# A two-layer graph network on one Trainium2 core: scatters without waits among themselves, an earlier clear of the sorted table, a smaller-stepped fill of the weights' table, deeper loads of terms

## Chip, cores and metric

The kernel runs on one core of a Trainium2 chip, as one launch. The metric is the device time of that core in microseconds; the figure for a kernel is the median over its runs. A profiled execution, recorded separately, gives the trace from which the views below are taken.

## What is computed

The reference has four parts, one after the other, on 6,250 nodes with 256 features and 100,000 edges sorted by destination:

```
x = x + GAT(layernorm(x), edges)            # 8 heads: softmax over incoming edges of exp(leaky_relu(..)), weighted sum
x = x + experts(layernorm(x))               # each node picks 1 of 32 experts: relu(relu(x W1 + b1) W2 + b2)
x = x + RGCN(layernorm(x), edges)           # T[n, rel] = x_n W_rel for 16 relations; sum over edges of T[src, rel] * weight
x = x + FFN(layernorm(x))                   # 2 of 8 experts, chosen once for all nodes, gelu, then a layer norm
```

The layer norms have no learned scale except the last one. Everything is float32.

## The kernel before

**Stages.** A preparation turns the edge lists into per-edge index columns. A *projection* loop over 13 blocks of four 128-node tiles (49 tiles in all) computes the attention projection and stores it in the DRAM table `H_tab`; the per-node terms of the destinations go to `ad_tab`. Then a long loop over 98 *groups* of 1,024 edges does the attention (GAT): GpSimd gathers the source rows of a group with eight indirect DMAs (`gather`, L444, tile `hs`, four buffers), SyncE (SP) loads the destination terms (`load_terms`, L476, four small DMAs per group into one of the tiles `aw`), ScalarE's queue loads the destinations (`load_dst`, tile `db`), and TensorE, VectorE (DVE) and ScalarE (ACT) turn them into sums in a ring of 16 tiles.

**The second layer runs inside the first.** The nodes are cut into three chunks of 6, 16 and 27 tiles. As soon as the ring holds finished sums, a chunk goes through four generators: `take` (normalise, write `x1_tab`), `route` (choose the expert, compute each node's slot in a table sorted by expert, scatter the rows there: L870, table `x_sort`), `experts` (load sorted rows and the expert's weights from `w_tab`, write `y_sort`) and `products` (gather back from `y_sort`, L952; multiply with the 16 relation matrices `wr`, L998; write `T_tab`, L1012). In each turn of the group loop `fill` runs a few steps of these, by a budget of TensorE and DVE time. A loop after the last group runs what is left. Then come the RGCN (98 groups, gathers from `T_tab`, also L444, tile `ts`) and the final FFN.

**What sets the order.** Group loop and remainder lie in `tc.manual_schedule()`: each engine and queue executes its instructions in the order in which the program wrote them.[...] Outside, a planner orders instructions by priority and readiness.

**What the change touches.** The scatters of `route`: 49 indirect DMAs on GpSimd, all writing `x_sort`; each source tile `xs2` (four buffers) is loaded from `x1_tab` by SP three tiles ahead (L113). The generator `Flow.consts`, of which one step runs per group: it fills `w_tab` (one row block per expert: W1, W2, b2 as the 65th row of the W2 part, b1 as last column, the rest zero), then clears `x_sort` (58 stores of 256 KB, four a step), then loads `wr`. `route` may scatter only when `self.ready` is set, after all clears. In `experts`, `ys` has two buffers. All three chunks share one `x_sort`, so a chunk waits until the one before has read its rows.

```
            for c in range(zero.shape[0] // P):
                nc.sync.dma_start(zero[c * P : (c + 1) * P, :], zr)
                if c % 4 == 3:
                    yield
            self.ready = True
```

Of the kernel before, what the change touches and what calls it, by code (L numbers as in the profile page):

```python
# [15 lines left out]
AX = mybir.AxisListType  # L16
DVE = mybir.EngineType.DVE
# [5 lines left out]
P = 128  # L23
# [6 lines left out]
T = 8  # L30
# [16 lines left out]
def gnn_ffn_kernel(  # L47
# [84 lines left out]
    nc.vector.memset(ones, 1.0)  # L132
    eps = const.tile([P, 1], F32, name="eps")
# [6 lines left out]
    dst_f = const.tile([P, T, NG], F32, name="dst_f")  # L140
# [22 lines left out]
    w_tab = dram.tile([E1, P, B1C + 4], F32, name="w_tab")  # L163
# [3 lines left out]
    class Chunk:  # L167


        def __init__(self, a, b, x_sort=None):  # L170
# [3 lines left out]
            if x_sort is None:  # L174
                self.x_sort = dram.tile([self.xt * P, 2 * D], F32, name=f"x_sort{a}_{b}")
            self.y_sort = dram.tile([self.xt * P, D], F32, name=f"y_sort{a}_{b}")
# [4 lines left out]
    whole = Chunk(0, NT)  # L181

# [41 lines left out]
    with tc.tile_pool(name="prep", bufs=1) as prep, tc.tile_pool(name="prep_p", bufs=1, space=PSUM) as prep_p:  # L224
# [72 lines left out]
        for a, o in ((dgf, dst_f), (srf, src_i), (i1f, idx1), (nat["ew"], ew_sb)):  # L297
            for h in range(2):
# [5 lines left out]
                if a is dgf:  # L304
                    nc.vector.tensor_tensor(
                        rlm[:, h * w : (h + 1) * w, :].rearrange("p (q u) g -> p q u g", u=QT),
                        pt.rearrange("p (q u) g -> p q u g", u=QT),
                        lo4[:, h * Q // 2 : (h + 1) * Q // 2, None, :].to_broadcast([P, Q // 2, QT, NG]), ALU.subtract)
                if h == 0:
# [38 lines left out]
    with tc.tile_pool(name="ga", bufs=2) as pa, tc.tile_pool(name="ga1", bufs=1) as pa1, \  # L348
# [16 lines left out]
        for t0, n, r in blocks:  # L365
# [16 lines left out]
            node_dma(nc.scalar, hb, H_tab, t0, n, r, True)  # L382

# [20 lines left out]
    class Group:  # L404


        def __init__(self, pool, g, dynamic):
# [9 lines left out]
            for o, a in ((ii[:, 0], src_i), (ii[:, 1], idx1), (fw[:, 0], dst_f), (fw[:, 1], ew_sb)):  # L417
                nc.vector.tensor_copy(o.rearrange("p (t o) -> p t o", o=1), a[:, :, ds(g, 1)])
            self.di = pool.tile([P, T], I32, name="d_di")
            nc.vector.tensor_copy(self.di, fw[:, 0, :])  # L420
# [38 lines left out]
        def load_dst(self):  # L459

            n = GE if self.dynamic else QT * P
            self.db = self.pool.tile([P, n], I32, name="db", bufs=1 if self.dynamic else 2)
# [191 lines left out]
    class Flow:  # L654


        def __init__(self, es, bufs, psum_bufs):

            self.open, self.bufs = 0, 1
            self.ready = False  # L660
# [13 lines left out]
        def consts(self, zero):  # L674

            yield
# [9 lines left out]
            zr = self.rt.tile([P, 2 * D], F32, name="xs2", bufs=4)  # L686
            nc.vector.memset(zr, 0.0)
# [4 lines left out]
            nc.sync.dma_start(w_tab.rearrange("e p w -> p e w"), zr[:, None, : B1C + 4].to_broadcast([P, E1, B1C + 4]))  # L692
            for k in range(KC):
                nc.sync.dma_start(w_tab[:, :, k * H1 : (k + 1) * H1], f1_w1[:, k * P : (k + 1) * P, :])
            nc.sync.dma_start(w_tab[:, :H1, W2C:B1C], f1_w2)
            nc.sync.dma_start(w_tab[:, H1, W2C:B1C], f1_b2)
            nc.sync.dma_start(w_tab[:, :H1, B1C], f1_b1)
            yield
            for c in range(zero.shape[0] // P):
                nc.sync.dma_start(zero[c * P : (c + 1) * P, :], zr)  # L700
                if c % 4 == 3:
                    yield
            self.ready = True
            for r in range(NREL):
                nc.sync.dma_start(self.wr[:, :, r, :], rel_w[r].rearrange("(k p) o -> p k o", p=P))
                if r % 2 == 1:
                    yield
# [50 lines left out]
        def route(self, ck):  # L758
# [94 lines left out]
            while not (ck.free() and self.ready):  # L853
# [14 lines left out]
            for j in range(ck.nt):  # L868
                r, xs2 = ahead.pop(0)
                nc.gpsimd.indirect_dma_start(  # L870
                    out=ck.x_sort[:, :], out_offset=bass.IndirectOffsetOnAxis(ap=ck.slot[:r, j : j + 1], axis=0),
                    in_=xs2[:r, :], in_offset=None)
                if j + 3 < ck.nt:
# [4 lines left out]
        def experts(self, ck):  # L878
# [7 lines left out]
            for s in range(np_ + 5):  # L886
                if 4 <= s < np_ + 4:
# [5 lines left out]
                    ys = pool.tile([P, 2, D], F32, name="ys", bufs=2)  # L893
# [24 lines left out]
                if 2 <= s < np_ + 2:  # L918
                    lv = live[s - 2]
                    for j in range(lv["n"]):  # L920
                        w = pool.tile([P, B1C + 4], F32, name="w", bufs=6)
                        nc.sync.dma_start(w, w_tab[ds(lv["e"][j], 1)].rearrange("o p w -> (o p) w"))
                        lv["w"].append(w)
                if s < np_:
# [3 lines left out]
                    nc.sync.dma_start(xs[:, :n, :], xs_rows[:, c : c + n, :])  # L928
# [120 lines left out]
    with ExitStack() as es_flow:  # L1049
# [6 lines left out]
        aws = [pr1.tile([P, Q, 2 * HEADS], F32, name=f"aw{i}") for i in range(3)]  # L1056
# [51 lines left out]
        with tc.manual_schedule():  # L1108

            boot = flow.consts(chunks[0].x_sort)  # L1110
            groups = [Group(pg, g, False) for g in range(NG)]
            for g in range(2):
                groups[g].load_dst()
# [264 lines left out]
```

## Time and profile before

| | us |
|---|---|
| median of 3 runs (3813.27 to 3839.88) | 3828.43 |
| the profiled execution, its own time | 3459.76 |
| its span, first to last instruction | 3458.0 |
| projection and preparation, to the first gather | 0 to 114.5 |
| GAT loop, from first to last gather of `hs` | 114.5 to 1287.9 |
| scatters of chunk 0; of chunk 1; of chunk 2 | 416 to 433; 786 to 848; 1358 to 1452 |
| experts of chunk 2, then its products | 1461 to 1600, then to about 2025 |
| RGCN gathers | 2026 to 3019 |
| final FFN | 3019 to 3458 |

The shares of busy time over the whole span (TensorE 70%, GpSimd 50%, DVE 31%, ACT 23%) hide that each stage has another limit. They are read by windows: the mean granted TensorE clock is 0.727 over the span, 1.00 in the products of chunk 2, and about 0.5 where TensorE waits a lot.

In the views, "PE" is TensorE's matmuls, "POOL" is GpSimd, a "q" behind an engine's name is its sequencer, and `x <- y` behind an idle time names what ended it. An indirect DMA counts as busy time of POOL[...]; the data land later.

### The profile page before, as it was taken

Reading aid. Unit: us, or ns where it says so; the run is one execution under the profiler, and the core shown is the slowest. Engines: PE = TensorE matmul, PEld = TensorE weight load, DVE = VectorE, ACT = ScalarE, POOL = GpSimd, SP = SyncE. Lnnn points to the kernel's source line nnn. Section 1 sums busy time; section 2 is a strip of 40 time slices with the busy share of each in tenths; the row PEclk is TensorE's granted clock in tenths of the full one; section 3 lists DMA queues with packets and bytes.
Section 4 is the critical chain, followed back from the end, with each engine's and each line's share of the span. In section 5 each row is a group of like instructions: output and inputs, shape, how many; then the busy total and the mean of one; then the engine's idle time right before and its main releaser. Section 6 shows DMA issues by size and latency. Waiting matters only on the chain. (4 is left out here: it accounts for less than half of the span.)

```text
span 3458.0 us, 32167 instructions
## 1 busy us (share of the span) xinstructions
PE 2423.5 (70%) x8917; PEld 1186.0 (34%) x8918; DVE 1069.1 (31%) x2879; ACT 803.6 (23%) x1684; POOL 1713.0 (50%) x1736
## 2 busy tenths in 40 slices
PE   5334457791675987188999966666666666689997
PEld 4212235341453443054444421111111111166665
DVE  7324646562555653011000002121121211242222
ACT  2112223440333443033333310000000000012332
POOL 0447676774757771200000047777777777622222
PEclk9655576885676999589999975555555555569999
DMA  4697687675886774586444453333333333310000
GB/s 146 193 217 244 186 278 229 200 227 177 265 264 186 227 219 161 169 264 219 168 171 170 159 188 105 105 105 105 105 105 105 105 105 105 89 28 19 19 19 20
DMA packets 326688, 533.40 MB, mean 154 GB/s; under 512 B 84966, under 2 KB 182564, under 8 KB 326496
## 3 DMA queue, kind: packets, MB, share of 16 engines
q1 hardware_dynamic: 218060, 277.92, 24.4%
q0 software_dynamic: 83152, 233.62, 23.7%
q10 hardware_dynamic: 25284, 19.67, 1.9%
q8 instruction: 75, 1.23, 0.2%
q14 instruction: 117, 0.96, 0.1%
HBM read 342.80 MB, written 192.42 MB: 155 GB/s over the span
## 5 line engine op out<-in xcount | busy, mean ns | idle before, releaser
L444 POOL DMA_INDIRECT hs<-H_tab,src_i x784 | 765.7, 977 | 428.3 <-issue 212.0
L444 POOL DMA_INDIRECT ts<-T_tab,idx x784 | 743.7, 949 | 330.4 <-issue 238.5
L998 PE MATMUL pb<-wr,xTt 128*128 128x512 f32 (+1 forms) x1568 | 722.2, 617 | 18.6 <-ACT tr L1001 14.1
L502 PE MATMUL qagg<-ts,oh 128*32 128x256 f32 x1568 | 504.6, 630 | 327.7 <-DMA ts<-T_tab,idx 324.0
L998 PEld LDWEIGHTS pb<-wr,xTt 128*128 128x128 f32 (+1 forms) x1568 | 303.9, 198 | 387.8 <-issue 356.7
L502 PEld LDWEIGHTS qagg<-ts,oh 128*32 128x32 f32 x1568 | 90.2, 139 | 719.9 <-DMA ts<-T_tab,idx 640.4
L1001 ACT COPY tr<-pb 128x512 f32<-128x512 f32 (+1 forms) x392 | 228.4, 587 | 452.7 <-PE pb L998 344.1
L509 ACT COPY qs<-qagg 128x264 f32<-128x264 f32 (+1 forms) x196 | 73.9, 377 | 1117.0 <-PE qagg L502 1095.3
L454 DVE TENSOR_TENSOR oh<-iota,rlm 128x256 f32<-128x256 f32 x196 | 83.1, 425 | 799.2 <-PE qagg L502 793.5
L518 PE MATMUL agg<-qs,pl 128*128 128x264 f32 (+1 forms) x392 | 204.4, 619 | 146.2 <-DVE pl L511 81.9
L557 PE MATMUL pe<-aw,oT 128*128 128x64 f32 x392 | 86.4, 362 | 296.2 <-issue 140.0
L952 POOL DMA_INDIRECT yg<-y_sort,slot x49 | 47.1, 961 | 489.0 <-ACT xl L717 291.6
L579 DVE TENSOR_TENSOR hs<-hs,pe 128x2048 f32<-128x2048 f32 x98 | 223.2, 2277 | 0.0
L557 PEld LDWEIGHTS pe<-aw,oT 128*128 128x128 f32 x392 | 76.5, 267 | 339.6 <-issue 247.9
L1328 PE MATMUL ph<-xT,we 128*128 128x512 f32 (+1 forms) x416 | 177.4, 584 | 15.1 <-DMA we<-in_L_ffn_W_dram,ix 11.7
L518 PEld LDWEIGHTS agg<-qs,pl 128*128 128x128 f32 x392 | 91.2, 280 | 270.5 <-ACT qs L509 162.6
L1336 PE MATMUL po<-we,hid 128*128 128x256 f32 (+1 forms) x784 | 171.9, 379 | 0.5 <-DVE we L1314 0.3
L1336 PEld LDWEIGHTS po<-we,hid 128*128 128x128 f32 (+1 forms) x784 | 148.4, 190 | 26.8 <-issue 5.7
L502 PE MATMUL qagg<-hs,oh 128*32 128x264 f32 x1568 | 155.7, 533 | 0.0
L894 DVE SCALAR_TENSOR_TENSOR ys<-pb,xs 128x512 f32<-128x512 f32 (+1 forms) x72 | 49.2, 684 | 324.8 <-PE pb L892 180.0
L904 PE MATMUL pb<-xTe,w 128*64 128x128 f32 x568 | 99.6, 326 | 40.1 <-DMA w<-w_tab 35.3
L915 PE MATMUL pt<-ident,xs 128*128 128x128 f32 x284 | 58.7, 341 | 95.6 <-DMA xs<-x_sort 92.7
(278 smaller groups left out, 2303.7 us busy)
## 6 DMA issues: line engine op xcount, KB each, us to landing
T_tab<-tr SPq DMA_DIRECT2D x384, 256.0 KB
xs<-x_sort SPq DMA_DIRECT2D x70, 512.0 KB
w<-w_tab SPq DMA_DIRECT2D x142, 194.0 KB
y_sort<-ys SPq DMA_DIRECT2D x70, 256.0 KB
x_sort<-xs SPq DMA_DIRECT2D x58, 256.0 KB
db<-in_dst_dram ACTq DMA_DIRECT2D x392, 32.0 KB
hs<-H_tab,src_i POOLq DMA_INDIRECT x784
ts<-T_tab,idx POOLq DMA_INDIRECT x784
```

The source lines that it names most:

```text
L444: nc.gpsimd.indirect_dma_start(out=hs[:, t, :], out_offset=None, in_=table, in_offset=bass.IndirectOffsetOnAxis(ap=idx(t), axis=0))
L454: nc.vector.tensor_tensor(oh, iota[:, None, :n].to_broadcast([P, T, n]), column(self.rl), ALU.is_equal)
L502: nc.tensor.matmul(ps[q * QW : (q + 1) * QW, :width], lhsT=oh[:, t, :], rhs=vals[:, t, :width], start=u == 0, stop=u == QT - 1)
L509: nc.scalar.copy(qs, ps[:, :width])
L518: nc.tensor.matmul(ps[:, :width], lhsT=pl, rhs=qs, start=True, stop=True)
L557: nc.tensor.matmul(pq[:, u * w : (u + 1) * w], lhsT=oT[:, u, :], rhs=aw.rearrange("p q h -> p (q h)"), start=True, stop=True)
L579: nc.vector.tensor_tensor(hv, hv, pv.to_broadcast([P, T, HEADS, HD]), ALU.mult)
L904: nc.tensor.matmul(ph[:H1, j * P : (j + 1) * P], lhsT=lv["w"][j][:, k * H1 : (k + 1) * H1], rhs=xT[:, k, j * P : (j + 1) * P], start=k == ...
L998: nc.tensor.matmul(pr[:r, :], lhsT=xT[:, k, j * P : j * P + r], rhs=self.wr[:, k, q0 : q0 + 2, :], start=k == 0, stop=k == KC - 1)
L1001: nc.scalar.copy(o2, pr[:r, :])
L1328: nc.tensor.matmul(ph[:, :nn], lhsT=we1[:, i, k, c * P : (c + 1) * P], rhs=xT[:, k, :nn], start=k == 0, stop=k == KC - 1)
L1336: nc.tensor.matmul(po[:r, :], lhsT=hid[:, i, c, j * P : j * P + r], rhs=we2[:, i, c, :], start=i + c == 0, stop=i + c == NFC)
```

## The change

Seven edits. (1) The 49 scatters are told not to depend on other scatters of the same chunk, and every load of sorted rows in `experts` is made to wait for all scatters of its chunk. (2) The written-out order of the group loop and of the remainder binds TensorE, DVE, ACT and SP, no longer GpSimd, whose instructions the planner places. (3) The clears of `x_sort` come from a constant tile of zeros, 128 columns wide and repeated four times along a row; three are issued in each block of the projection, one more along with each load of a relation matrix, and the rest after these. `route` asks for as many cleared tiles as its chunk has. (4) `w_tab` is not zeroed; it is filled in eight steps, two for each quarter of the experts (8 of 32). The rows below the 64 used ones get copies of W2 and b1, and b2 then overwrites one of them. Its rows are 385 columns, not 388. (5) Terms `aw` have six tiles, not three, and are loaded four groups ahead, not two; destinations `db` have three buffers, loaded three groups ahead. (6) `ys` has three buffers. (7) `dst_f`, used only in a branch for wide groups, is not kept; the branch loads it from DRAM.

```diff
@@ constants @@
+    zeros = const.tile([P, P], F32, name="zeros")
+    nc.vector.memset(zeros, 0.0)
-    dst_f = const.tile([P, T, NG], F32, name="dst_f")
-    w_tab = dram.tile([E1, P, B1C + 4], F32, name="w_tab")
+    w_tab = dram.tile([E1, P, B1C + 1], F32, name="w_tab")
@@ new class @@
+    class Clear:
+        def __init__(self, table):
+            self.rows, self.n, self.done = table.rearrange("(c p) (k w) -> c p k w", p=P, w=P), table.shape[0] // P, 0
+        def step(self, n):
+            for c in range(self.done, min(self.done + n, self.n)):
+                nc.sync.dma_start(self.rows[c], zeros[:, None, :].to_broadcast([P, 2 * D // P, P]))
+            self.done = min(self.done + n, self.n)
+    cleared = Clear(chunks[0].x_sort)
@@ projection, end of a block @@
             node_dma(nc.scalar, hb, H_tab, t0, n, r, True)
+            cleared.step(3)
@@ load_dst @@
-            self.db = self.pool.tile([P, n], I32, name="db", bufs=1 if self.dynamic else 2)
+            self.db = self.pool.tile([P, n], I32, name="db", bufs=1 if self.dynamic else 3)
@@ Flow.consts @@
-            nc.sync.dma_start(w_tab.rearrange("e p w -> p e w"), zr[:, None, : B1C + 4].to_broadcast([P, E1, B1C + 4]))
-            for k in range(KC):
-                nc.sync.dma_start(w_tab[:, :, k * H1 : (k + 1) * H1], f1_w1[:, k * P : (k + 1) * P, :])
-            nc.sync.dma_start(w_tab[:, :H1, W2C:B1C], f1_w2)
-            nc.sync.dma_start(w_tab[:, H1, W2C:B1C], f1_b2)
-            nc.sync.dma_start(w_tab[:, :H1, B1C], f1_b1)
-            yield
-            for c in range(zero.shape[0] // P):
...
-            self.ready = True
+            for e in range(0, E1, E1 // 4):
+                es = slice(e, e + E1 // 4)
+                for k in range(KC):
+                    nc.sync.dma_start(w_tab[es, :, k * H1 : (k + 1) * H1], f1_w1[es, k * P : (k + 1) * P, :])
+                nc.sync.dma_start(w_tab[es, :H1, W2C:B1C], f1_w2[es])
+                yield
+                nc.sync.dma_start(w_tab[es, H1:, W2C:B1C], f1_w2[es])
+                nc.sync.dma_start(w_tab[es, H1, W2C:B1C], f1_b2[es])
+                for rows in (slice(0, H1), slice(H1, P)):
+                    nc.sync.dma_start(w_tab[es, rows, B1C], f1_b1[es])
+                yield
             for r in range(NREL):
                 nc.sync.dma_start(self.wr[:, :, r, :], rel_w[r].rearrange("(k p) o -> p k o", p=P))
-                if r % 2 == 1:
-                    yield
+                clear.step(1)
+                yield
+            while clear.done < clear.n:
+                clear.step(1)
+                yield
@@ route @@
-            while not (ck.free() and self.ready):
+            while not (ck.free() and self.clear.done >= ck.xt):
                 yield None
...
-                nc.gpsimd.indirect_dma_start(
+                ins = nc.gpsimd.indirect_dma_start(
                     out=ck.x_sort[:, :], out_offset=bass.IndirectOffsetOnAxis(ap=ck.slot[:r, j : j + 1], axis=0),
                     in_=xs2[:r, :], in_offset=None)
+                ck.put.append(ins.ins)
+                tc.declare_no_dep(ins.ins, group=ck.key, reason="no two nodes share a slot")
+                tc.add_to_no_dep_group(ck.key, ins.ins)
@@ experts @@
-                    ys = pool.tile([P, 2, D], F32, name="ys", bufs=2)
+                    ys = pool.tile([P, 2, D], F32, name="ys", bufs=3)
...
-                    nc.sync.dma_start(xs[:, :n, :], xs_rows[:, c : c + n, :])
+                    ins = nc.sync.dma_start(xs[:, :n, :], xs_rows[:, c : c + n, :])
+                    for put in ck.put:
+                        tc.add_manual_dep(ins.ins, put.name, mybir.DependencyInfo(
+                            mybir.DependencyClass.Sync, mybir.DependencyReason.DATA), reason="all rows are there")
@@ group loop @@
-        aws = [pr1.tile([P, Q, 2 * HEADS], F32, name=f"aw{i}") for i in range(3)]
+        aws = [pr1.tile([P, Q, 2 * HEADS], F32, name=f"aw{i}") for i in range(6)]
-        with tc.manual_schedule():
+        with tc.manual_schedule(engines={PE, DVE, ACT, SP}):
...
-            for g in range(2):
-                groups[g].load_dst()
-                groups[g].load_terms(aws[g % 3])
+            for g in range(4):
+                if g < 3:
+                    groups[g].load_dst()
+                groups[g].load_terms(aws[g])
...
-                if g + 2 < NG:
-                    groups[g + 2].load_dst()
-                    groups[g + 2].load_terms(aws[(g + 2) % 3])
+                if g + 3 < NG:
+                    groups[g + 3].load_dst()
+                if g + 4 < NG:
+                    groups[g + 4].load_terms(aws[(g + 4) % 6])
...
-        with tc.manual_schedule():
+        with tc.manual_schedule(engines={PE, DVE, ACT, SP}):
             while takes or routes or runs or tails:
```

## Prediction

> **What bounds the kernel now.** The whole-span shares decide nothing here, so I read the busy time by stages first, cutting at the scatters that the timeline of GpSimd shows. Columns: stretch, its length, then busy time and count for PE, weight loads, DVE, ACT and POOL, the granted clock, DMA share, GB/s.
>
> ```profile
> 177.00:213.00 36.00, 3.01 (x20) 1.53 (x20) 0.31 (x1) 0.31 (x2) 0.89 (x2) 0.50 1.10 155
> 213.00:416.00 203.00, 101.14 (x542) 53.86 (x542) 117.54 (x250) 52.39 (x131) 154.47 (x160) 0.54 0.76 234
> ...
> 786.00:848.00 62.00, 10.97 (x68) 5.62 (x68) 8.50 (x16) 3.97 (x13) 22.87 (x24) 0.57 0.50 153
> ...
> 1358.00:1461.00 103.00, 20.27 (x38) 8.34 (x38) 0.59 (x4) 6.28 (x11) 26.60 (x27) 0.58 0.45 148
> 1461.00:1600.00 139.00, 114.83 (x510) 73.76 (x511) 19.86 (x33) 43.44 (x103) 0.00 (x0) 0.86 0.84 265
> 1600.00:2025.00 425.00, 416.11 (x1018) 186.56 (x1016) 22.39 (x120) 162.97 (x295) 26.25 (x27) 1.00 0.45 165
> ```
>
> From 213 to 416 GpSimd issues 160 gathers in 203 us, 1.27 us each, while PE, DVE and ACT are busy half the time or less: the rate of gathers sets the pace. In three stretches (177 to 213, 786 to 848, 1358 to 1461) no engine does much. Next the table of waits (total, times, longest):
>
> ```profile
> POOL x_sort L870 <- DMA x_sort<-xs,slot: 102.1, 41, 3.7
> ...
> PE pe L557 <- DMA aw<-ad_tab: 80.7, 7, 44.4
> DVE ys L894 <- DMA y_sort<-ys: 78.8, 14, 9.8
> ...
> POOL hs L444 <- PE qagg L502: 73.8, 18, 35.1
> ```
>
> Every scatter waits for the one before, 102.1/41 = 2.49 us each. The timelines place the others:
>
> ```profile
> 209.54 1.09 PE L557 MATMUL pe<-aw,oT 128*128 128x64 f32 x4 [44.44 <-DMA aw<-ad_tab]
> ...
> 212.93 1.01 POOL L444 DMA_INDIRECT hs<-H_tab,src_i  x1 [35.11 <-PE qagg L502]
> ...
> 1358.23 0.99 POOL L870 DMA_INDIRECT x_sort<-xs,slot  x1 [39.15 <-DVE le L850]
> 1362.15 0.98 POOL L870 DMA_INDIRECT x_sort<-xs,slot  x1 [2.93 <-DMA x_sort<-xs,slot]
> 1365.63 0.96 POOL L870 DMA_INDIRECT x_sort<-xs,slot  x1 [2.50 <-DMA x_sort<-xs,slot]
> ```
>
> At 209 TensorE has waited 44 us for terms that SP queued behind the fill of `w_tab`; GpSimd then lacks free `hs` buffers for 35 us. From 1358 all 27 scatters of chunk 2 stand on the path: the experts cannot begin before them, and after the experts TensorE is full (416 of 425 us), so time won here reaches the end. The RGCN (784 gathers over 993 us) and the final FFN are not touched.
>
> **What the Trainium skill says.** "DMA: Bandwidth & Descriptors", section "Anatomy of one DMA — SWDGE (gpsimd) path", puts some 2 us of fixed cost on such a DMA, most of it confirmation of the write. The trace agrees: 2.0 to 3.7 us between the end of one scatter's issue and the next. The section "Two DMAs through the same engine are not ordered" says that only a completion semaphore orders two transfers; hence the loads of sorted rows must still wait for all scatters. The trace has that wait (SP at L928, 36.4 us in 3 waits). The section "Why a DMA increments its semaphore by 16 and not by 1" says that a transfer uses the largest number of engines up to 16 that divides the outer dimensions: quarters of 8 experts would run on 8 engines where 32 gave 16. No run so far shows such a transfer.
>
> **The parts, in us of the profiled execution.**
>
> *Chunk 2's scatters.* First to last start: 1358.23 to 1450.38, 92.2 us for 26 steps, 3.54 each. Without the wait a step cannot be shorter than GpSimd's 0.96 + 0.30 = 1.26, so 33 us. The next limit is `xs2`: four buffers, each loaded (SP issue 0.4; landing about 2, an estimate from the scatter's like wait), scattered (0.96) and landed (2.5) before reuse: about 6 us by four is 1.5 a step, 39 us. SP also puts `T_tab` stores between loads, and two of these held it 4 us each (1382.8 to 1387.0, 1411.2 to 1415.5). I take 44: **48 saved**, bounds 35 and 58.
>
> *Start of the loop.* Terms now go four groups ahead, ahead of all filling. The wait of 35.1 should go; I take **28**, bounds 8 and 35. What may return is the fill: it loses 6.2 MB of zeros, gains 2 MB of copies, and becomes 28 DMAs instead of 6. Before, W1, W2 and b2 held SP's queue from 175.67 to 198.2 with 4 MB. On half the engines, with copies, that may be 22.5 x 2 x 1.5 = 68 us of queue, and each b2 row waits for the copy it overwrites (four times perhaps 6). Spread over eight groups of 10 us, some 90 us stands against 80; four groups of lead cover the 10 us deficit. If the cover fails, TensorE waits for `aw` again; that is the lower bound.
>
> *Scatters of chunks 0 and 1.* Chunk 0: 416.34 to 432.30 is 16.0 for 5 steps, 6.3 at 1.26. Chunk 1: 61.3 for 15 steps and 8 gathers in between, 29.0 at 1.26. Excess 9.7 + 32.3 = 42. Gathers may now fill gaps. The `xs2` limit keeps a part if they do not: 20 x 0.25 = 5. I take **34**, bounds 15 and 42.
>
> *Experts of chunks 0 and 1.* GpSimd waits for `qagg` 14.9 us between 434 and 600 and 22.6 us between 848 and 1060; in the same windows DVE waits 23.0 and 22.5 for stores of `ys`. A third `ys` buffer and `db` one group earlier (same 392 DMAs on ACT) remove the DVE wait, not the matmuls. **18**, bounds 0 and 38. *Experts of chunk 2:* the remaining 78.8 - 45.5 = 33 us of that wait lie in a stage where DMA runs at 0.84 and 265 GB/s, so I take **4**, bounds 0 and 15; next late are the loads.
>
> *Clears.* 13 blocks x 3 = 39 stores move to the projection: 39 x 0.26 MB = 10.2 MB. SP issues one in 0.42 us, 16 us in all, with only 14 `xin` loads of 0.4 us and four edge loads beside it. At the 265 GB/s seen in the experts they are 39 us of DMA, 32 at its share of 0.84. The first 30 us have a DMA share of 0.28 and the next 85 of 0.48, so 66 us are free: they fit. In pieces of 512 B they may be slower. Placed early, they delay the first `xin`; placed late, the last `H_tab` stores. Cost **6**, bounds 0 and 35. Where they leave the loop GpSimd was the limit anyway, so nothing is gained there; the cover is GpSimd's 1.27 us a gather. The relation loads, one a group, are the same 16.
>
> *The rest:* two copies of `dst_f` (about 0.5 us each by like rows) against one memset; rows of 385 columns, 1% less to load; the wait of the sorted loads for all scatters was there already. Nothing.
>
> Sum: 48 + 28 + 34 + 18 + 4 - 6 = **126**, against the profiled 3459.76: about 3334. The median of the timed runs is 369 us above that execution, and the profile doesn't show where. If TensorE runs slower there, the GAT loop is nearer to TensorE's limit and the terms inside it are worth less, while those at 177 and 1358, where TensorE idles, stay. I carry the sum over nearly whole: 3828 - 123 = **3705**.
>
> **The rivals.**
>
> *The consumers bind.* In the GAT loop PE is 80 to 88% busy from 1060 to 1290 (185 of 230 us). If the loop runs at PE's and DVE's pace, waits of GpSimd are only exchanged for waits on `hs` buffers, and of the loop's 80 us about 6 remain. For: 18 waits on `qagg` exist already. Against: in 213 to 416 and at 786 PE starves. Time: 48 + 6 + 4 - 6 = 52, 3776.
>
> *The change is hidden or does not act:* if scatters still wait (for the shared semaphore, or for `xs2`), 28 + 18 + 4 - 6 = 44 remain, 3784.
>
> *More:* all upper bounds but half, no cost of clears: about 180, 3648.
>
> *Slower.* GpSimd's order is no longer written out, and it is the stage's bound, so any wait that the planner puts in front of gathers goes straight to the end. There are 14 such places in the loop: three batches of scatters and about eleven pairs of `yg` gathers. The trace shows what such an instruction waits when its partner is not ready: 39.15 us (on `le`) and 26.5 us (`yg` on `xl`), today after the last gather, where nothing is queued behind. At 12 us a place the loss is 168, net 42: 3870. It decides from 126/14 = 9 us a place, about one group. For: planner and chip may differ. Against: today these places wait 0.3 us, and with a written order gathers are just as stuck.
>
> **How the numbers follow.** Chances: forecast 0.58, more 0.07, consumers bind 0.17, does not act 0.07, slower 0.11. The range 3630 to 3805 takes in the forecast's bounds and the two weaker gains; beyond it lie the slower case and a little of the better one. The measurement tells about 1% (38 us) from no change. Faster by over 1%, below 3790: nearly all of the forecast and more (0.64), and most of the two weak cases (0.17), 0.81. Slower by over 1%, above 3867: half of the slower case and a tail of unpriced effects, 0.09. Within: 0.10.
>
> **What would show it.** Scatters of chunk 2 about 1.5 us apart; the wait of L870 on scatters near zero; no 35 us gap of GpSimd before 215; last `hs` gather near 1215; TensorE idle less than 45 us before the experts of chunk 2; first gather before 121. The forecast is wrong if waits of `hs` on `qagg` grow by what L870 loses, if GpSimd waits before `yg` or a scatter with gathers behind it, or if the first gather comes after 140.

## The result and the profile after

The kernel after takes 3768.49 us (median of 4 runs, 3767.10 to 3778.74) where before takes 3825.55 (4 runs): a ratio of 0.9855, interval 0.9816 to 0.9895. The gain is 57 us; 123 were forecast.

Two kinds of chip have to be kept apart first, because they answer differently. On **kind A** before takes 3818 to 3828 us (medians): all timed runs up to this result, and the trace of after. On **kind B** it takes 3448 to 3460: the profiled execution that the prediction was worked from belongs here. Each chip showed one kind only, but none served at two times, so the chip and the occasion are not told apart. Every ratio below is against before on the same chip. One late run of before (e16) fell on kind A, its span 3816.3, so the change can be followed there in a pair of traces. The pair on B is e1 (before) and e5 (after). A group of edges is marked by the start of ScalarE's copy of its sums (`qs`), read from the traces.

| us from the start | A before | A after | difference | B before | B after | difference |
|---|---|---|---|---|---|---|
| first gather of `hs` | 114.7 | 120.7 | +6 | 114.7 | 118.0 | +3 |
| group 0 | 173.6 | 184.7 | +11 | 157.5 | 168.1 | +11 |
| group 3 | 235.7 | 216.7 | -19 | 217.1 | 185.8 | -31 |
| group 12 | 341.3 | 341.7 | 0 | 297.3 | 300.7 | +3 |
| group 56 | 918.7 | 928.6 | +10 | 780.7 | 796.0 | +15 |
| group 60, past chunk 1's scatters | 1029.9 | 1015.9 | -14 | 877.1 | 891.4 | +14 |
| last gather of `hs` | 1490.7 | 1474.1 | -17 | 1276.5 | 1297.9 | +21 |
| first scatter of chunk 2 | 1594 | 1573 | -21 | 1349 | 1375 | +26 |
| last scatter of chunk 2 | 1686 | 1630 | -56 | 1442 | 1431 | -11 |
| last store of `T_tab` | 2246.1 | 2198.1 | -48 | 2004.9 | 2000.3 | -5 |
| span | 3816.3 | 3765.5 | -51 | 3440.0 | 3435.7 | -4 |

The scatters of chunk 2 give 35 to 37 us on both kinds, the experts after them take 6 to 8 back, and the loop, from which 80 us were expected, gives 17 on A and costs 21 on B. Single traces of one kernel differ too: with the two other traces of before on B, the loop there costs 11 or 16, not 21, and e1's is the fastest of its 18 executions, e5's the slowest of its four. So the B columns show the change too poor by some 10 us; timed, after gains 14.5 us on B.

The same reading by stages as in the prediction, kind A. Columns: stretch, length, then busy time and count of PE, weight loads, DVE, ACT and POOL, granted clock, DMA share, GB/s. First before: start of the loop, chunk 1's scatters, chunk 2's scatters, its experts, its products.

```profile
180.00:236.00 56.00, 8.51 (x44) 4.06 (x44) 8.78 (x15) 3.83 (x11) 18.05 (x20) 0.50 0.98 209
...
910.00:973.00 63.00, 16.05 (x96) 8.11 (x96) 13.65 (x25) 6.30 (x18) 22.67 (x24) 0.59 0.48 160
...
1594.00:1687.00 93.00, 19.46 (x38) 8.02 (x36) 0.21 (x1) 6.13 (x11) 25.91 (x27) 0.59 0.46 158
1687.00:1827.00 140.00, 108.24 (x524) 70.47 (x524) 20.61 (x34) 43.99 (x104) 0.26 (x1) 0.91 0.83 270
1827.00:2246.00 419.00, 414.81 (x1005) 185.27 (x1002) 21.70 (x119) 161.54 (x293) 26.19 (x27) 1.00 0.45 166
```

Then after:

```profile
184.00:217.00 33.00, 13.31 (x74) 6.08 (x66) 12.98 (x22) 5.50 (x17) 22.14 (x24) 0.50 0.45 110
...
918.00:986.00 68.00, 15.86 (x80) 7.19 (x76) 17.30 (x33) 7.62 (x21) 48.13 (x49) 0.58 0.61 191
...
1573.00:1631.00 58.00, 18.63 (x38) 7.85 (x38) 0.81 (x5) 6.18 (x11) 26.09 (x27) 0.68 0.78 255
1631.00:1780.00 149.00, 113.08 (x525) 73.03 (x526) 20.56 (x34) 44.81 (x106) 0.53 (x1) 0.88 0.81 256
1780.00:2198.00 418.00, 414.29 (x1002) 184.97 (x1001) 21.69 (x119) 161.15 (x291) 26.26 (x27) 1.00 0.47 166
```

The idle start is shorter, chunk 1's scatters share their stretch with gathers (49 instructions of GpSimd in 68 us, not 24 in 63), chunk 2's take 58 instead of 93. The experts need 149 instead of 140. Now the waits of GpSimd inside the loop (total, times, longest), before and then after:

```profile
POOL hs L444 <- PE qagg L502: 134.1, 20, 30.8
...
POOL x_sort L870 <- DMA x_sort<-xs,slot: 42.4, 17, 4.7
```

```profile
POOL hs L464 <- PE qagg L522: 179.8, 32, 20.8
```

The wait among scatters is gone, and the wait for free `hs` buffers has grown by 45.7 where 42.4 went. On B the wait for `hs` grows from 70.4 to 115.3, by 44.9, for 40.8 lost. The prediction named exactly this as the sign against it. It is not an exchange place by place, though: of what the `hs` buffers took on A, two long waits stand at chunk 0's scatters (16.4 us at 530) and behind chunk 1's (18.3 at 1004), and the rest is spread over many small ones.

### The profile page after: what moved, and what is told of

Same layout as the page of the kernel before. It is cut to its first block, busy times and chain, and to the rows that moved or that the text cites. A ratio compares the mean times of both kernels' runs of the same rounds, so it can differ in the third digit from the quotient of the medians.

```text
span 3765.5 us, 32026 instructions
## 1 busy us (share of the span) xinstructions
PE 2129.9 (57%) x8917; PEld 1161.6 (31%) x8918; DVE 1067.1 (28%) x2881; ACT 798.6 (21%) x1683; POOL 1717.9 (46%) x1736
## 5 line engine op out<-in xcount | busy, mean ns | idle before, releaser
L1026 PE MATMUL pb<-wr,xTt 128*128 128x512 f32 (+1 forms) x1568 | 730.0, 621 | 51.5 <-issue 26.0
L522 PE MATMUL qagg<-ts,oh 128*32 128x256 f32 x1568 | 191.9, 617 | 21.0 <-DMA ts<-T_tab,idx 19.4
L1358 PE MATMUL ph<-xT,we 128*128 128x512 f32 (+1 forms) x416 | 176.8, 582 | 16.4 <-DMA we<-in_L_ffn_W_dram,ix 12.9
L546 DVE SCALAR_TENSOR_TENSOR ring<-agg,win,ring 128x264 f32 x196 | 96.6, 493 | 186.7 <-PE agg L538 74.1
L546 DVE SCALAR_TENSOR_TENSOR acc<-agg,win,acc 128x256 f32 x196 | 94.3, 481 | 150.0 <-issue 44.1
L919 DVE SCALAR_TENSOR_TENSOR ys<-pb,xs 128x512 f32<-128x512 f32 (+1 forms) x72 | 49.2, 683 | 263.6 <-PE pb L917 210.0
```

What stands on the lines that cost most here:

```text
L522: nc.tensor.matmul(ps[q * QW : (q + 1) * QW, :width], lhsT=oh[:, t, :], rhs=vals[:, t, :width], start=u == 0, stop=u == QT - 1)
L546: nc.vector.scalar_tensor_tensor(a, ps[:, :width], self.win(w), a, op0=ALU.mult, op1=ALU.add)
L1026: nc.tensor.matmul(pr[:r, :], lhsT=xT[:, k, j * P : j * P + r], rhs=self.wr[:, k, q0 : q0 + 2, :], start=k == 0, stop=k == KC - 1)
L1358: nc.tensor.matmul(ph[:, :nn], lhsT=we1[:, i, k, c * P : (c + 1) * P], rhs=xT[:, k, :nn], start=k == 0, stop=k == KC - 1)
```

## The experiments

All kernels compute the whole result. In short, medians, each against before on its chip (e1 to e4 shared a chip, and so did e5 to e8, e9 to e12, e13 to e15, and e16 to e18):

| run | kind | us | ratio, interval |
|---|---|---|---|
| e1 before again | B | 3447.69 | 0.9997, 0.9990 to 1.0004 |
| e5 after again | B | 3434.65 | 0.9957, 0.9940 to 0.9974 |
| e2 scatters wait again | B | 3494.43 | 1.0127, 1.0110 to 1.0144 |
| e3 as e2, GpSimd ordered too | B | 3459.39 | 1.0029, 1.0020 to 1.0039 |
| e4 clears in the loop | B | 3450.05 | 0.9999, 0.9989 to 1.0009 |
| e6 fill by rows | B | 3422.39 | 0.9924, 0.9907 to 0.9941 |
| e7 three scatters a step | B | 3412.66 | 0.9888, 0.9872 to 0.9905 |
| e8 before, three a step | B | 3460.78 | 1.0031, 1.0020 to 1.0041 |
| e9 e6 and e7 together | A | 3720.40 | 0.9746, 0.9730 to 0.9762 |
| e10 two `ys` buffers | A | 3768.10 | 0.9868, 0.9852 to 0.9885 |
| e11 terms two ahead | A | 3737.39 | 0.9806, 0.9757 to 0.9855 |
| e12 scatters' edit alone | A | 3752.45 | 0.9819, 0.9796 to 0.9843 |
| e14 router's weights first | B | 3430.06 | 0.9914, 0.9889 to 0.9940 |
| e17 the same | A | 3748.38 | 0.9821, 0.9795 to 0.9847 |
| e15 e6, e7 and e14 together | B | 3403.95 | 0.9835, 0.9810 to 0.9861 |
| e18 as e15, terms two ahead | A | 3700.70 | 0.9693, 0.9670 to 0.9716 |

e13 and e16 are before once more, for traces (3452.66 on B, 3818.09 on A).

**Which chip (e1, e5, e13, e16).** No edit.

> The kernel before, unchanged, to see a second trace of it. Theory: the first trace of it, 3458 us, was an uncommon execution, and the timed runs near 3825 are slower because TensorE answers late (the copy qs of the changed kernel starts up to 20 us after the last matmul by the record); then this trace has a span of 3800 to 3840, an RGCN stage of about 1110 us instead of 993, and waits of GpSimd's gathers ts on a releaser that the trace does not name of 100 us or more. Rival: the late answers came with the change; then this trace is like the first, 3440 to 3480.

> The changed kernel, unchanged, beside a kernel before that runs at 3450 or at 3825. Theory: where TensorE answers promptly (before near 3450) the change is worth nothing: the run with the clears in the loop was equal to the kernel before, so this is 3445 to 3475, ratio 0.999 to 1.007; where before is near 3825 the ratio is 0.985 again. Rival: the ratio is 0.985 on every chip, because the early clears win what the run with the clears in the loop lacked.

> Before, unchanged, for a trace beside the next two. Theory, if the chip answers like that of the last four runs: a span of 3810 to 3830, chunk 2's first scatter at 1545 to 1575 and its last at 1640 to 1665, TensorE's wait for the router's weights 13 to 16 us where after had 28.7. Rival: the loop of before is longer there (first scatter of chunk 2 after 1590), and the change gained in the loop too. On a chip of the other kind: as in the first run, 3440.

> Before, unchanged, for a trace beside the next two. Theory, on the chip where before takes 3817: span 3810 to 3830, first scatter of chunk 2 at 1545 to 1575, its last at 1640 to 1665, TensorE's wait for the router's weights 13 to 16 us. Rival there: first scatter after 1590, so that the change gained in the loop too. On the other kind: 3440 to 3455 again, and nothing new.

The theory of e1 fell: before is not bound to the long time, it took 3447.69 on that chip. Its rival had the number right, but not the reason, as e16 shows below. e5 lay between its two answers: 14.5 us of gain, neither none nor 50. e13 fell on B and told nothing new. e16 fell on A and gave the pair of traces above; its first scatter came at 1594, where its rival had it: the change gains in A's loop too, 17 us between these two traces. Where A loses its 370 us is seen in the largest waits of the two runs of after. Kind A:

```profile
ACT qs L529 <- remote: 1110.7, 95, 38.5
DVE oh L474 <- remote: 844.9, 95, 35.4
```

and kind B (e5):

```profile
ACT qs L529 <- PE qagg L522: 1128.2, 184, 12.4
DVE oh L474 <- PE qagg L522: 805.3, 166, 14.2
PEld qagg L522 <- DMA ts<-T_tab,idx: 637.9, 391, 3.6
```

On B ScalarE copies the sums when TensorE's last matmul of the group ends, and TensorE waits for gathered rows. ("Remote" is an event that the profile can put down to no instruction.) On A the copy starts up to 28 us after the modelled end of that matmul, in the RGCN over 2 us late in 71 of 98 groups, 757 us in sum. Before has the same there (70 groups, 760 us), so the change isn't its cause. The RGCN takes 1110 us on A, 979 on B. The packets of its gathers are not slower: 148 to 150 ns each on average on A, 148 on B. What makes TensorE go on late on those chips isn't settled by any run here.

**The scatters' waits and GpSimd's order (e2, e3, e12).** e2 takes the first two lines out, e3 also writes GpSimd's order out again (no run has edit 1 with that order written out):

```diff
-                tc.declare_no_dep(ins.ins, group=ck.key, reason="no two nodes share a slot")
-                tc.add_to_no_dep_group(ck.key, ins.ins)
...
-        with tc.manual_schedule(engines={PE, DVE, ACT, SP}):
+        with tc.manual_schedule():
```

e12 is before with edits (1) and (2) only.

> The changed kernel, with the scatters of a chunk waiting for each other again; GpSimd's order stays free. Theory: the scatters of chunk 2 carry most of the 57 us gained, so this is 45 to 70 us slower than the changed kernel, 3815 to 3840, ratio to before 0.995 to 1.003. Rival: the gain came from the start of the loop and the deeper loads; then it stays below 3795.

> As the run with waiting scatters, and GpSimd's order is written out again too. Theory: the free order is worth nothing in itself, so this is within 10 us of the run with waiting scatters. Rival: the planner's order puts scatters or gathers of products in front of gathers that are ready, costing 20 us or more; then this is faster than it by that.

> Before with only the scatters' edit: no waits among the scatters of a chunk, sorted loads behind all of them, GpSimd's order free. All other edits left out. Theory (parts add: after without this edit took 10 us more than before, after with it 15 us less): 25 us faster than before, ratio 0.990 to 0.995, chunk 2's scatters in 56 us instead of 92, chunk 1's still about 60 with a TensorE stall of over 45 us in it. Rival A (the scatters' waits are worth their 60 us, the other edits spoil it): ratio 0.985 or below. Rival B (freeing GpSimd's order costs in the loop what chunk 2 gains): 0.998 or above.

e2 is 60 us slower than after, as expected. But e3, expected within 10 of e2, is 35 us faster, as its rival said: with waiting scatters, the planner's order of GpSimd costs 35 us against the written one. So edit 2 has a price of its own that the prediction had only as a rival. Of the 60 us of e2, edits 1 and 2 together keep 25 (e3 against after). e12, 25 us expected, gained 65, but it fell on A, where it beats the whole change by 16 us (on the chip of e12 the change was run with two `ys` buffers, as e10, and takes 3768.10 too). That is what its rival A said.

Taken together these runs say which edits gain. Edits 3 to 7 alone cost 10 us on B (e3 against before), and added to edits 1 and 2 they cost 16 on A (e12 against after). All of the gain is from the scatters' edits: 25 on B, 65 on A.

The price of the free order stands where scatters meet the loop. At chunk 0, groups 24 to 26 take 66 us in e2 and 46 in e3: TensorE waits there for the sorted rows, which wait for all six scatters, now mixed with gathers. (Columns of such lines: start, length, engine, line, operation, output and inputs, count, and in brackets the idle time before and what ended it.) First e3, then e2:

```profile
431.82 1.09 PE L938 MATMUL pt<-ident,xs 128*128 128x128 f32 x4 [21.55 <-DMA xs<-x_sort]
```

```profile
455.59 1.09 PE L938 MATMUL pt<-ident,xs 128*128 128x128 f32 x4 [42.84 <-DMA xs<-x_sort]
```

In after, where the scatters don't wait, this stop is 26.2 us, with one of 8.0 behind it, against 22.8 in before (B). The other place is chunk 1, groups 56 to 60: 109 us in e2, 97 in e3. The planner puts the 16 scatters among 32 gathers, four groups' worth. TensorE's longest idle time there, kind B, before (e1):

```profile
818.12 1.22 PE L518 MATMUL agg<-qs,pl 128*128 128x264 f32 x2 [29.62 <-ACT oT L486]
854.54 1.22 PE L518 MATMUL agg<-qs,pl 128*128 128x264 f32 x2 [30.99 <-DVE pl L511]
```

and after (e5), with DVE and SP:

```profile
877.02 1.08 PE L577 MATMUL pe<-aw,oT 128*128 128x64 f32 x4 [58.08 <-issue]
```

```profile
873.50 1.23 DVE L771 SCALAR_TENSOR_TENSOR xr<-xr 128x1024 f32<-128x1024 f32 x1 [51.35 <-DMA xr<-in_x_dram]
```

```profile
794.90 35.88 SPq L114 DMA_DIRECT2D xs<-x_tab  x8
...
836.82 16.10 SPq L114 DMA_DIRECT2D xs<-x_tab  x5
...
870.00 0.40 SPq L114 DMA_DIRECT2D xr<-in_x_dram  x1
```

Two stops of 30 us have become one of 58 (73 in e2). SP's order is still written out: eight loads of rows for scatters stand in a row, and each needs one of four buffers, hence a scatter that has landed. GpSimd now runs those scatters between gathers, so SP takes 36 us for eight loads, and the load of `xr` for the next take, behind them, is issued at 870. DVE waits 51 us for it, and TensorE, for whose wait of 58 the profile names no releaser, goes on 3.5 us after DVE does. On A TensorE's stops there are 17.6 and 36.5 us in after (DVE's wait for `xr` 29.9) and were 26.0, 32.2 and 19.7 in before: 54 for 78. That fits the gain of chunk 1, groups 56 to 60: 111 us, then 87, on A; 96, then 95, on B, where 58 stand for 61.

**Three scatters a step (e7, e8).** If that chain is right, fewer loads in a row must shorten it.

```diff
-                if j % 8 == 7:
+                if j % 3 == 2:
```

> The changed kernel, with a step of route ending after three scatters, not eight. Theory: the batch of chunk 1 stalls TensorE 58 us because SP's stream has eight loads of xs2 in a row, each waiting for a scatter that GpSimd runs between gathers, and the load of xr for the next block, on which DVE waits, is behind them; with three a step no wait of TensorE between the groups 55 and 66 exceeds 25 us, and this is 20 to 50 us faster than the changed kernel. Rival: GpSimd's extra instructions are the limit there, and the same time is spread out: within 10 us.

> The kernel before, with a step of route ending after three scatters. Theory: here each scatter waits for the one before on GpSimd, but a group of gathers stands between two batches, so SP's loads seldom wait; 20 to 50 us faster than the kernel before, ratio 0.985 to 0.994. Rival: scatters that wait still cost GpSimd 2.5 us each, in whatever place: within 10 us of before.

After gains 22 us by it; TensorE's stop falls to 38.8, with one of 12 ahead of it, so not below the 25 that was also expected. The same line in before costs 12 us, where 20 to 50 of gain were expected. The trace of e8 shows where it loses: at group 60 it is 10 us or more ahead of every trace of before on B, but chunk 2's scatters take 102 us instead of 92, and the rest of the loop is longer. In after (e7) they take 61 instead of 56. So a smaller step helps at chunk 1's place in both kernels, and its price at chunk 2 is less where the scatters don't wait. That fits the chain for chunk 1; why before loses more isn't shown further.

**The start of the loop (e6, e11, e14, e17).** e6 fills each eighth by a quarter of the rows of all 32 experts instead of all rows of 8 experts:

```diff
-            for e in range(0, E1, E1 // 4):
-                es = slice(e, e + E1 // 4)
+            for i in range(4):
+                p, h = P // 4, H1 // 4
...
-                    nc.sync.dma_start(w_tab[es, :, k * H1 : (k + 1) * H1], f1_w1[es, k * P : (k + 1) * P, :])
+                    nc.sync.dma_start(w_tab[:, i * p : (i + 1) * p, k * H1 : (k + 1) * H1],
+                                      f1_w1[:, k * P + i * p : k * P + (i + 1) * p, :])
```

> The changed kernel, with each fill step taking a quarter of the rows of all 32 experts instead of all rows of 8 experts: same bytes, same eight steps, but 32 in the outer dimension; the row of b2 is overwritten once, not four times. Theory: the fill ran on half of the DMA engines, and TensorE's 57 us of waits for terms between 165 and 345 come from it and from the waits of SP for the copies; they fall below 25 us and group 12 is done 10 to 25 us earlier. Later stages take a part back: 0 to 20 us faster than the changed kernel. Rival: the waits come from the gathers' own traffic; then nothing moves.

It gains 12 us. TensorE's waits for terms between 165 and 345 fall from 60 us to 36, not below the 25 expected, and group 12 comes 9 us earlier. In after two steps of the fill come round every 27 us (SP's first loads of a quarter start at 205.6, 232.7 and 259.2 in e5) where the gathers of two groups take 20, and the lead seen at group 3 is gone by group 12. By rows, the fill ends and the loads of `wr` begin at 275 instead of 286. That agrees with what the prediction cited from the Trainium skill ("DMA: Bandwidth & Descriptors", section "Why a DMA increments its semaphore by 16 and not by 1": with 8 experts outermost a transfer gets 8 engines), though no view shows the number of engines, and with the shorter chain of overwritten b2 rows too: one wait of 4.3 us for a copy before b2 where after had four, 20.3 in sum. The run doesn't part the two.

e11 undoes edit 5; e14 and e17 keep it but move three loads:

```diff
             self.clear = clear
+            nc.sync.dma_start(self.gb, row_bcast(gat_bias, D))
+            nc.sync.dma_start(self.rb, row_bcast(router_b, E1))
+            rw = self.rt.tile([E1, D], F32, name="xs2", bufs=4)
+            nc.sync.dma_start(rw, router_w)
             yield
+            yield
...
             boot = flow.consts(cleared)
+            next(boot)
```

> After with three tiles of terms, loaded two groups ahead, and two destination buffers loaded two ahead. Theory (the depth wins 30 us at group 3 and the fill takes them back by group 12): group 3 later by 20 to 30 us, group 24 within 8 us of after, the whole 0 to 8 us slower than after, ratio 0.995 to 0.999. Rival (without the depth TensorE waits for terms behind every fill step): 25 us slower or more, ratio 1.003 or above, with waits for terms of over 100 us in the first 12 groups.

> After with the router's weights, its bias and the GAT bias loaded ahead of the first terms instead of behind them; nothing else moved. Theory (deeper terms put eight more small loads in front of the router's weights on SP, and TensorE's transposes of these stand in front of the groups): the wait of the transposes gone (under 3 us where after had 16.3 or 28.7), group 0 earlier by 12 to 25 us, the kernel 10 to 25 us faster than after: ratio 0.977 to 0.983 on the chip where after has 0.9855, 0.989 to 0.993 where it has 0.9957. Rival (GpSimd's gathers or the fill catch up by group 12): within 5 us of after.

> After with the router's weights, its bias and the GAT bias loaded ahead of the first terms, once more. Theory on the chip where after has 0.9855: group 0 earlier by 20 to 28 us, ratio 0.977 to 0.981, so most of what undoing the depth won (0.9806). Rival there: 0.983 or above, so the depth costs in another way. On the other kind: 0.989 to 0.993 again.

Without the deeper terms the kernel is 31 us faster on A, outside both expectations (31 by the medians; one of e11's four executions took 3766, as long as after). Group 3, expected 20 to 30 us later, came at 210.9, 6 us earlier than in after. So the 19 us that after wins at group 3 on A are not won by the depth. e12, which lacks edits 3 to 7, has group 3 at 234.2, as before; what is left to win them is most likely the fill in small steps, in place of one block of stores and loads ahead of the terms, though no run has it alone. On B no run undoes the depth.

TensorE's waits tell what the depth costs. The transposes of the router's weights (L708; L690 in before) stand in TensorE's order ahead of the first group's sums, and SP issues their load behind the terms. Before on A, then after on A:

```profile
167.37 0.39 PE L690 MATMUL pb<-ident,xs 32*128 32x32 f32 x2 [22.36 <-DMA xs<-in_L_ffn_router_w_dram]
```

```profile
178.50 0.39 PE L708 MATMUL pb<-ident,xs 32*128 32x32 f32 x2 [28.68 <-DMA xs<-in_L_ffn_router_w_dram]
```

and what SP issues ahead of it in after:

```profile
139.53 31.13 SPq L496 DMA_DIRECT2D aw<-ad_tab  x20
170.77 0.41 SPq L114 DMA_DIRECT2D xr<-in_x_dram  x1
171.69 2.75 SPq L496 DMA_DIRECT2D aw<-ad_tab  x4
174.87 0.36 SPq L702 DMA_DIRECT2D gb<-in_L_gnn_bias_dram  x1
175.29 0.42 SPq L703 DMA_DIRECT2D rb<-in_L_ffn_router_b_dram  x1
175.76 0.43 SPq L705 DMA_DIRECT2D xs<-in_L_ffn_router_w_dram  x1
```

Edit 5 put eight more loads of terms there, 1.56 us each on A (31.13/20), 0.82 on B (20 in 16.31). The router's weights are issued 11 us later than in before on A and 10 on B, and group 0 comes 11 later on both. Of that, 6 us on A and 3 on B are the later start of the terms, behind the clears; only the rest is the eight loads.

With the router's weights first that wait is gone, and group 0 comes at 154 instead of 168 on B. What the whole kernel gains by it there is between 5 and 13 us: e14 is 27.9 us faster than before, where after was 14.5 faster, but they ran on two chips on which before differs by 9 us, and e14's own time is only 4.6 below that of after. So theory (10 to 25) and rival (within 5) are not told apart on B. On A, e17 is 20 us faster than after by the times, 13 by the ratios, and its 0.9821 lies between theory and rival; TensorE there still stands 16.9 us at the same place, with the wait put down to terms.

A further part of e11's gain comes between groups 12 and 16: 60.5 us in after, 49.2 in e11. TensorE stands there for 19.1 us in after, and DVE ahead of it waits 11.8 for a store of `x_tab`, which SP issues between loads of terms. In e11 TensorE's longest stop there is 9.2, with no such wait of DVE above 5. The traces of e9 and e17, which have the depth, and of e18, which has not, agree: 60.3, 63.7 and 47.4 us. On A, then, the depth costs at this place too; by which loads it makes the store late was not tested alone.

**The clears (e4).** All 58 go to the loop again, four a step behind the fill; `wr` two a step.

```diff
-            cleared.step(3)
...
+            while clear.done < clear.n:
+                clear.step(4)
+                yield
```

> The changed kernel, with all 58 clears back in the group loop, four a step after the weights' table, and two relation matrices a step. Theory: the clears cost 6 us ahead of the first gather (120.7 against 114.5) and win nothing, so this is 0 to 10 us faster than the changed kernel, 3758 to 3770. Rival: clears in the loop slow the gathers' landings and the terms; then it is 15 us or more slower.

15 us slower than after, so the rival had the size right: the first gather comes 3.7 us earlier, but groups 12 to 24 take 128.7 us instead of 111.6. The mechanism is not the rival's. 13 of the 17 us are one stop of TensorE, 33.8 us instead of 20.7, and DVE ahead of it waits for the same store of `x_tab`, 25.1 us instead of 12.9:

```profile
337.54 0.76 DVE L767 TENSOR_TENSOR xr<-ring,den 128x256 f32<-128x256 f32 x2 [25.06 <-DMA x_tab<-xr]
```

In e4 SP issues that store at 331.65, behind four clears in every group. The early clears are worth their place.

**The third `ys` buffer (e10).**

```diff
-                    ys = pool.tile([P, 2, D], F32, name="ys", bufs=3)
+                    ys = pool.tile([P, 2, D], F32, name="ys", bufs=2)
```

> After with two ys buffers instead of three. Theory (the third buffer only exchanged a wait for stores for a wait for the weights' loads): within 4 us of after (ratio to before 0.994 to 0.998 where after has 0.9957), the wait of DVE for stores of ys back near 70 us, TensorE's wait for w back near 30. Rival (the third buffer is worth a good part of the 63 us of wait that it removed): 12 us slower than after or more, ratio 0.999 or above.

3768.10, the same as after. With two buffers, then with three (after), kind A:

```profile
DVE ys L919 <- PE pb L917: 135.1, 21, 78.8
...
DVE ys L919 <- DMA y_sort<-ys: 63.1, 13, 10.6
...
PE pb L929 <- DMA w<-w_tab: 42.6, 25, 15.1
```

```profile
DVE ys L919 <- PE pb L917: 210.0, 43, 77.0
...
PE pb L929 <- DMA w<-w_tab: 68.2, 38, 15.2
```

63 us of wait for stores become 75 more for matmuls, which wait 26 more for weights. An exchange, in which the kernel gains nothing. That the experts of chunk 2 are 6 to 8 us longer in after is not due to the buffer either: from the last scatter to the last store of `y_sort` they take 157 us with two, 154 with three. It may be no effect at all, as three traces of before on B have 150.5, 154.9 and 157.3.

**Together (e9, e15, e18).**

> After with both: the weights' table filled by quarters of rows of all 32 experts, and three scatters a step instead of eight. Theory (the two lie at different places, start of loop and groups 50 to 66, and what GpSimd wins reaches the end): the gains add, 12 and 22 us against after, so about 3400 us where before takes 3449: ratio 0.982 to 0.989, and the last gather of hs at 1255 to 1270. Rival (after groups 12 to 40 the loop catches up by itself, so an early gain is lost again): no better than three a step alone, ratio 0.988 to 0.993, last gather about 1275.

> After with the fill by quarters of rows, three scatters a step, and the router's weights ahead of the terms. Theory (gains at different places add): 10 to 25 us less than fill by rows and three a step had together, ratio 0.967 to 0.973 on the chip where those had 0.9746, about 0.978 to 0.985 on the other. Rival: no better than those two, 0.974 or above (0.985 on the other).

> The fill by rows, three scatters a step and the router's weights first, with terms and destinations two groups ahead as in before. Theory (with the router's weights out of the way the depth covers the fill, and undoing it costs 3 to 12 us): 0.984 to 0.988 on the chip where the three with the depth had 0.9835, 0.968 to 0.974 on the other kind. Rival (the depth itself costs, small loads in front of others on SP): 10 us faster than the three, 0.981 or below, or 0.965 or below.

The gains add for the most part. On A the fill by rows and three a step bring 48 us against after, more than the 34 they had apart on B; the last gather came at 1436, a figure that the expectation had only for B. With the router's weights first, e15 gains 54 us on B where after gains 14.5: 40 more, where the three apart had 12, 22 and 5 to 13. e18, on A, gains 120 us of before, twice the change's own 57, and is the best kernel measured there. Whether the depth is worth keeping on B, beside the moved load, isn't known: e15 and e18 ran on different kinds.

## Why the prediction had the direction and not the size

It forecast faster by over 1%, and so it is on A; the size was off by 66 us. The direction owes something to luck: the prediction was worked from a trace of kind B, and on B the gain is 0.4%. What failed is what it gave for edits 3 to 6: 28 + 18 + 4 - 6 = 44 us to gain, where edits 3 to 7 cost 10 us (e3, B) and 16 (e12, A). The scatters, 48 + 34 = 82, brought 65 on A and 25 on B. By its own steps, with the pair of traces on A (B in brackets):

- *Chunk 2's scatters, 48 (35 to 58).* 35 (37): the right place, at the lower bound. The term mis-sized is the reuse of `xs2`, put at 6 us by four buffers. The trace shows GpSimd still waiting 24.9 us in 16 waits, now for loads:

```profile
1590.87 0.96 POOL L891 DMA_INDIRECT x_sort<-xs,slot  x1 [1.71 <-DMA xs<-x_tab]
1593.19 0.96 POOL L891 DMA_INDIRECT x_sort<-xs,slot  x1 [1.36 <-DMA xs<-x_tab]
```

  56.5 us for 26 steps is 2.17 a step, so a buffer comes round in 8.7 us.
- *Start of the loop, 28 (8 to 35).* 19 (31) at group 3, nothing at group 12. This is **the step that failed first**: "Terms now go four groups ahead, ahead of all filling" took the depth for what wins and left out what is queued behind these loads on SP, the router's weights and the stores of `take`. On A the depth won nothing at group 3 and its undoing made the kernel 31 us faster (e11). And "four groups of lead cover the 10 us deficit" was too kind about the fill: "some 90 us" was forecast, and on B its eight steps, with loads of terms among them, took from 158.6 to 286.0, 127 us, in which TensorE waited 60 us for terms.
- *Scatters of chunks 0 and 1, 34 (15 to 42).* Chunk 1 gave 24 (1), chunk 0 about 2 (a loss of 13, groups 24 to 26). Here **"Gathers may now fill gaps"** failed: they do, and that holds back the last landings. At chunk 0 it is the sorted rows that come late to TensorE, at chunk 1 SP's loads and at last `xr`.
- *Experts of chunks 0 and 1, 18 (0 to 38); of chunk 2, 4.* Nothing by the third buffer; chunk 2's lost 8 (6), which is within what traces of before differ by on B.
- *Clears, -6.* The first gather is later by 6.0 (3.3), as priced; moved back they cost 15.
- *The rest, 0.* From the end of chunk 2's products to the end of the run 3 us more are gained on A, none on B.

The three loop terms, 80 us, thus came to 23 on A (17 at the last gather, after the 6 that the clears cost ahead of it) and to a loss of 8 to 18 on B. The rival "the consumers bind" foretold 52 us and 3776, close to the 51 of the spans and 3768, and its sign, the exchanged waits, is there within 4 us. That is in part luck, as its reason was another: TensorE and DVE were not full, they stood waiting for sorted rows and for SP. The rival "slower" was right that a free order has a price, 35 us in e2 against e3. But it came at two of its 14 places, some 21 us at chunk 0's scatters and 13 at chunk 1's, and not as GpSimd waiting before a scatter: the gathers were held because TensorE had not freed their buffers. One reading of the first lines was too round as well: from 213 to 416 DVE is busy 58%, not half the time or less.

The step from the profiled 3460 to the timed 3828 was across two kinds of chip, which the prediction could not see. Carrying the sum over nearly whole was not what failed: chunk 2's term came out the same on both, and the loop did better on A than on B.

## What to carry to other kernels

When loads are moved ahead on a queue with a written order, list what they overtake and which engine stands still for the last of those: eight small loads made group 0 later here by 5 to 7 us because one matmul waited behind them. Look at a mark well behind the start: 19 to 31 us won at group 3 were gone at group 12. Undo each part of a bundle alone: undoing one edit of seven won 31 us on A. And where one engine's order is set free while the others stay written out, search the written queues for waits on the free engine: part of the wait removed on GpSimd came back at the `hs` buffers, through the sorted rows at chunk 0 and through SP, DVE and TensorE at chunk 1.

## What was not expected of the hardware

The same kernel takes 11% longer on some chips: 3818 against 3449. Gathers are issued alike (0.95 us and 0.30 between), chunk 2's products take as long, from the last store of `y_sort` to the last of `T_tab` 414 us on A and 413 on B, but TensorE's answers come up to 28 us late in the RGCN, and SP needs 1.56 us a load of terms at the loop's start instead of 0.82. A scatter that need not wait for another is issued 1.26 us after it at the soonest (chunk 0 of e5), and 3.5 on average when it must (chunk 2 of before).
